# Queries and keys by seven block products instead of eight, in a transformer block on one core

## The chip, the cores and the metric

The kernel runs on one core of one Trainium2 chip, in one launch. The metric is the device time of one execution in microseconds (us), as the median of several runs. The engines are called by the names of the profile: PE (TensorE, matrix products; PEld is its weight load), DVE (VectorE), ACT (ScalarE), POOL (GpSimd), SP (SyncE, which issues nearly all transfers).

## The reference

Everything is float32. The input `h` is 8 sequences ("batches" below, b = 0 to 7) of 1024 tokens with 512 channels.

```
x = h
x = x + layernorm(attention(layernorm(x)))       # 16 heads of 32, causal
x = x + layernorm(ffn(layernorm(x)))             # 512 -> 2048 -> 512

attention:  q, v, k = split(x @ Wqvk)            # each 1024 x 512
            s = (q k^T + causal mask) / sqrt(512), per head
            wv = softmax(s) v;  result = wv @ Wo
ffn:        hidden = x @ W1 + b1
            act = relu(hidden + c * w_imag * sin(theta + 0.1 hidden) * 0.1)
            result = act @ W2 + b2                # c = cos(theta) w_real + sin(theta) w_imag
```

## The kernel before, in words

One program goes through the 8 batches one after the other. Inside a batch come attention, then the feed-forward part, and the two are interlocked: a batch's first norm, its first projections and its moments are made while the batch before is still at work. The order of instructions on every engine is the order in which the program emits them (`in_order`), and Python generators say where work is slipped in: `advance(work)` emits the next step of a generator, `finish(work)` the rest.

The normalised input of a batch lies transposed in two tiles `xnT[b, 0]` and `xnT[b, 1]`, one for each half of 512 tokens, each with four chunks (`kc`) of 128 channels. Heads are handled in four groups of four (g = 0 to 3); a group has 128 columns of queries, of keys and of values.

**Projections of a group** (`project_qkv`, line 461). Queries and keys come from `queries_or_keys(n, half)`: four matmuls of 128x512 (the four chunks) into one PSUM bank, evacuated by ACT at line 488. Four such calls make 16 matmuls (line 477). In the profile one float32 matmul is two records. Values come from `values(t0)`, line 497: eight matmuls of 128x128 for two token tiles, and an ACT copy; four calls. These steps are the filler: the attention of group g is interleaved with the projections of the group after it (after g = 3: of group 0 of the next batch).

**Attention of a group** (`attention`, line 770) has three stretches.

1. `find_maxima` (line 536) needs row maxima. It has four runs. A run is PE score matmuls (line 575), which DVE reduces straight from PSUM (lines 593 and 605). Run 0 has one unit, runs 1 to 3 have two; a unit takes four of the eight PSUM banks. After each run come filler steps, as many as `MAX_FILL` says (its first row is for g = 0). The partial maxima are cut into bf16 parts (`split`, lines 553 to 562) and transposed on PE (line 115).
2. The first part of the second pass, three units of keys for queries 0 to 511 (`at` = 0, 1, 2). At `at` 0 and 1, `later` runs the two late units of maxima, called here the late runs A and B (`MAX_LATE`). A unit of the second pass is `weigh`: bf16 matmuls that subtract the maxima (line 681), score matmuls (line 692) into four banks, an ACT exponential for each half of them (line 707), and on diagonal blocks a POOL `affine_select` (line 711). One unit later `weighted_values` (line 730) multiplies with the values.
3. The second part, seven units for queries 512 to 1023 (`at` = 3 to 9; u = 0 to 6). DVE adds up the weights (line 759), for the sums that are taken at the next group's run 0 (line 745). A filler step comes after the `weigh` of u = 5 and one after that of u = 6: they are the first two half-steps of the projections after next.

During g = 2, PE also transposes the next batch's norm (`norm1`, two tiles at `at` = 0 and 1 and at u = 5 and 6); during g = 3 the output projection (line 897) is slipped in from `at` = 4 on.

**PSUM.** `psum()` hands out banks by a fixed rule when the program is built: of the free banks or pairs, the one that was drained longest ago in program order. A unit of maxima or of the second pass takes two pairs.

**Feed-forward** (`feed_forward`, line 942) has eight steps s of seven products (line 1009) with DVE and ACT work on their results, and a second layer (line 1144) whose operands POOL prepares (line 1125); it ends with s = 7 and a tail s = 8 in which the second layer alone is left.

Of the kernel before, what the change touches and what calls it, by code (L numbers as in the profile page):

```python
# [32 lines left out]
def kernel(  # L33
# [22 lines left out]
    TPB = HALF // P  # L56
    HPG = P // HD
    NG = NH // HPG
    QSCALE = 1.0 / math.sqrt(D)

    HC = HPG // 2
    MPART = 3
# [48 lines left out]
    def in_order(instruction):  # L111
        tc.keep_in_program_order(instruction)
# [19 lines left out]
    PRODUCTS2 = ("2", "4", "1", "6", "7", "5", "3")  # L132
    w1_mixed = dram.tile([NSTEP, len(PRODUCTS), P, 2 * 2 * P], F32, tag="w1m", name="w1_mixed")
    w2_mixed = dram.tile([NSTEP, len(PRODUCTS2), P, 2 * QUART], F32, tag="w2m", name="w2_mixed")
    wqvk_v = w_qvk.rearrange("(kc p) n -> p kc n", p=P)

    def w_tile(shape, name):
# [257 lines left out]
    def norm1_first():  # L395

        dst = new_xnT(0)
        return staged(NT, *norm_stages(lambda t: xt[0, t], dst, nc.scalar.copy))

    moments_ahead = {}  # L400

    def measure_ahead(b, steps):
# [58 lines left out]
    def project_qkv(b, g):  # L461

        if g and g + 1 < NG:
            fetch(b, g + 1)
        elif g + 1 == NG and b + 1 < B:
            fetch(b + 1, 0)
        qk[b, g] = [pp.tile([P, S], F32, tag="p", name=f"{n}_{b}_{g}") for n in "qk"]  # L470
        v[b, g] = pp.tile([P, NT, P], F32, tag="p", name=f"v_{b}_{g}")

        def queries_or_keys(n, half):
            pq = psum([P, HALF])
            for kc in range(KC):
                in_order(
                    nc.tensor.matmul(  # L477
                        pq,
                        w_of[b, g, 2 * n][:, kc, :],
                        xnT[b, half][:, kc, :],  # L480
                        start=(kc == 0),
                        stop=(kc == KC - 1),
                    )
                )
# [3 lines left out]
            in_order(nc.scalar.activation(dst, pq, AF.Copy, scale=1.0 if n else -QSCALE))  # L488
            drained(pq)
            yield True  # L490

        def values(t0):
            pv = psum([P, 2, P])
            for t in (t0, t0 + 1):
                for kc in range(KC):
                    in_order(
                        nc.tensor.matmul(  # L497
                            pv[:, t - t0, :],
                            xnT[b, t // TPB][:, kc, (t % TPB) * P : (t % TPB + 1) * P],
                            w_of[b, g, 1][:, kc, :],  # L500
                            start=(kc == 0),
                            stop=(kc == KC - 1),
                        )
                    )
            in_order(nc.scalar.copy(v[b, g][:, t0 : t0 + 2, :], pv))
            drained(pv)
            yield True

        yield from queries_or_keys(0, 0)
        yield from values(0)  # L510
        yield from queries_or_keys(1, 0)
        yield from queries_or_keys(0, 1)
        yield from queries_or_keys(1, 1)
        for t0 in (2, 4, 6):
            yield from values(t0)

    MAX_RUNS = (  # L520
        (((0, 0), (2, 0)),),
# [248 lines left out]
    def attention(b, wvT, after):  # L770
# [23 lines left out]
        work = projections(0)  # L794
        for g in range(NG):
            more, first = after(g)
            mT, later = find_maxima(b, g, work, sums, more if first is None else iter(()))
            mTs = [mT]
            at = 0
            for c in range(2):  # L800
                accs = []
                total = None
                units = KEY_UNITS[c]
                for u, keys in enumerate(units):
                    later(at)
# [26 lines left out]
                    def step(accs=accs, u=u, last=u == len(units) - 1, weights=weights, c=c, g=g,  # L832
                             placed=placed, total=total, apart=c and apart, dst=wvT[c][:, g, :]):
                        if u == 0:
                            accs.append(psum([P, HALF]))
                        acc = accs[0]
                        weighted_values(acc, b, g, u == 0, last, weights, placed)
                        if apart:
                            if not last:
                                accs.append(psum([P, HALF]))  # L840
                                weight_sums(accs[1], *total, last=False)
                            weight_sums(accs[1], weights, placed, first=False, last=last)
                        if last and c:

                            def whole():
                                if apart:
                                    whole_sum = accs[1]
                                else:
                                    whole_sum = psum([P, HALF])
                                    weight_sums(whole_sum, *total)  # L850
                                divide(acc, whole_sum, dst)

                            summing[0] = whole
                        elif last:
                            nc.scalar.copy(dst, acc)
# [15 lines left out]
    def finish_block(b, half, wvT, x2T, mixed, out_w):  # L871


        x2T[half] = tp.tile([P, KC, HALF], F32, tag="t", name=f"x2T_{b}_{half}")
        mixed[half] = mixp.tile([P, 3, 2, QUART], F32, tag="mix", name=f"mix_{b}_{half}")
        ys, xns, mvs, rss = {}, {}, {}, {}

        def x(t):
# [46 lines left out]
        def mix(t):  # L925
# [6 lines left out]
            m1, m2, m4 = (mixed[half][:, n, :, t * P : (t + 1) * P] for n in range(3))  # L932
# [9 lines left out]
    def feed_forward(b, x2T, mixed, before, between):  # L942
# [49 lines left out]
        def product(bank, s, name, first=False):  # L992
# [7 lines left out]
                "4": m[:, 2],  # L1000
                "5": m[:, 0],
                "6": m[:, 1],
# [247 lines left out]
        load(WEIGHTS - 2 - KC)  # L1250
        advance(between)
        finish(before)
        units = second()
        advance(units)
        for s, quota in enumerate(SECOND):
# [3 lines left out]
            for n, more in enumerate(quota):  # L1259
# [19 lines left out]
    for _ in range(TPB):  # L1279
# [76 lines left out]
```

## Time and profile before

| | |
|---|---|
| median of 3 runs (lowest, highest) | 3681.59 us (3681.03, 3681.76) |
| the profiled execution's own time | 3681.3 us |
| its span in the trace | 3679.6 us |
| granted PE clock | 0.997 |
| PE busy | 3601.1 us, 98% |
| DVE busy | 2680.4 us, 73% |
| ACT busy | 1408.2 us, 38% |
| POOL busy | 1133.8 us, 31% |
| DMA | 476.21 MB, mean 129 GB/s |

Busy times are of one profiled execution. Its own time is 1.7 us more than its span and 0.3 us under the median. The ends of matmuls are modelled, so the starts of successive PE groups say more than their durations: what a block of matmuls takes is read from its start to the start of the next block. A batch takes about 460 us, some 230 us of it attention.

### The profile page before, as it was taken

How to read it: one execution, taken by the hardware profiler on the slowest of the kernel's cores; microseconds unless marked ns; L12 is line 12 of the kernel's file. 1: busy time of each engine (PE TensorE's matmuls, PEld its weight loads, DVE VectorE, ACT ScalarE, POOL GpSimd, SP SyncE). 2: the span in 40 equal slices, each digit the busy share in tenths (PEclk: the TensorE clock that was granted, in tenths of full speed). 3: DMA queues.
4: the chain of work that ended last, by engine and by line, in shares of the span. 5: the costliest groups of instructions: out<-in, count | busy, mean ns of one | idle time of the engine just before them, and what ended most of it. 6: DMA issues, size and time to landing. Idle time of an engine off the chain costs nothing.

```text
span 3679.6 us, 61558 instructions
## 1 busy us (share of the span) xinstructions
PE 3601.1 (98%) x22721; PEld 2357.4 (64%) x22721; DVE 2680.4 (73%) x5571; ACT 1408.2 (38%) x2708; POOL 1133.8 (31%) x1740
## 2 busy tenths in 40 slices
PE   8999999999999999999999999999999999999998
PEld 4447864478654786548854488544885458854587
DVE  5877867678676786767867678776787767777775
ACT  4552135621355213652146521465114642156410
POOL 2333432134311343113431234222342223422243
PEclk9999999999999999999999999999999999999999
DMA  4444751047510574105841068310683116820176
GB/s 137 142 141 132 243 192 34 20 146 249 175 41 10 158 258 154 41 10 172 266 132 41 13 185 269 112 41 18 198 275 92 38 33 199 262 70 13 47 220 197
DMA packets 305084, 476.21 MB, mean 129 GB/s; under 512 B 29136, under 2 KB 90640, under 8 KB 304784
## 3 DMA queue, kind: packets, MB, share of 16 engines
q1 hardware_dynamic: 302624, 470.44, 40.8%
q8 instruction: 181, 2.97, 0.3%
q10 hardware_dynamic: 2160, 1.84, 0.2%
q14 instruction: 119, 0.97, 0.1%
HBM read 440.70 MB, written 31.46 MB: 128 GB/s over the span
## 4 chain that ended last, share of the span: by engine, by line
PE 83%; DVE 11%; ACT 2%; POOL 2%; issue 1%; DMA 0%; POOLq 0%; DVEq 0%; SPq 0%; ACTq 0%
PE banks L1144 16%; PE banks L1009 15%; PE banks L477 13%; PE banks L575 8%; PE banks L730 7%; PE banks L692 7%; PE banks L497 7%; PE banks L897 6%; PE banks L681 3%; PE banks L115 2%; DVE u L1036 2%; DVE hid L1052 2%; DVE u L1030 1%; PE banks L745 1%; DVE hid L1058 1%; ACT w L707 1%
## 5 line engine op out<-in xcount | busy, mean ns | idle before, releaser
L707 ACT ACTIVATE w<-banks 128x1024 f32<-128x1024 f32 (+1 forms) x640 | 566.6, 939 | 296.1 <-PE banks L692 296.0
L759 DVE TENSOR_TENSOR w<-w 128x1024 f32<-128x1024 f32 (+3 forms) x400 | 421.9, 1099 | 186.7 <-PE banks L730 151.8
L711 POOL TENSOR_SCALAR_AFFINE_SELECT w<-w 128x256 f32<-128x256 f32 x512 | 287.3, 578 | 847.2 <-ACT w L707 839.8
L605 DVE CUSTOM_DVE_ANT_0 es<-banks,mask 128x128 f32<-128x128 f32 (+3 forms) x1024 | 432.5, 485 | 102.6 <-PE banks L575 102.6
L1009 PE MATMUL banks<-x2T,wm 128*128 128x256 f32 x2048 | 477.3, 381 | 28.1 <-DVE u L1079 13.6
L477 PE MATMUL banks<-xnT,wqvk 128*128 128x512 f32 x1024 | 481.3, 609 | 0.7 <-ACT xnT L342 0.7
L1144 PE MATMUL banks<-wm,hm 128*128 128x256 f32 x2048 | 470.4, 380 | 2.3 <-POOL hm L1125 2.3
L1037 ACT ACTIVATE u<-u 128x1024 f32<-128x1024 f32 x128 | 135.3, 1057 | 852.1 <-DVE u L1036 803.5
L1009 PEld LDWEIGHTS banks<-x2T,wm 128*128 128x128 f32 x2048 | 386.7, 190 | 91.0 <-DVE u L1079 16.8
L1144 PEld LDWEIGHTS banks<-wm,hm 128*128 128x128 f32 x2048 | 388.0, 190 | 56.4 <-POOL hm L1125 5.5
L593 DVE TENSOR_REDUCE mx<-banks 128x1 f32<-128x512 f32 (+1 forms) x384 | 309.8, 862 | 109.1 <-PE banks L575 109.1
L1144 PE MATMUL banks<-wm,hid 128*128 128x256 f32 x1536 | 357.7, 379 | 0.0
L1009 PE MATMUL banks<-mix,wm 128*128 128x256 f32 x1536 | 354.6, 380 | 2.3 <-DVE u L1079 2.3
L1125 POOL TENSOR_TENSOR hm<-hid 128x256 f32<-128x256 f32 x256 | 204.0, 797 | 456.2 <-DVE hid L1058 437.9
L477 PEld LDWEIGHTS banks<-xnT,wqvk 128*128 128x128 f32 x1024 | 182.8, 190 | 239.1 <-issue 184.5
L692 PE MATMUL banks<-q,k 32*128 32x512 f32 (+3 forms) x3072 | 329.6, 491 | 0.0
L730 PE MATMUL banks<-w,v 128*32 128x512 f32 (+3 forms) x3072 | 318.5, 495 | 5.4 <-POOL w L711 5.4
L1009 PEld LDWEIGHTS banks<-mix,wm 128*128 128x128 f32 x1536 | 291.1, 190 | 50.6 <-issue 7.6
L575 PE MATMUL banks<-k,q 32*128 32x512 f32 (+3 forms) x3072 | 322.0, 513 | 0.4 <-DVE mx L605 0.2
L1144 PEld LDWEIGHTS banks<-wm,hid 128*128 128x128 f32 x1536 | 292.4, 190 | 39.1
L625 ACT ACTIVATE es<-es,mx 128x512 f32<-128x512 f32 (+3 forms) x512 | 279.6, 550 | 2.1 <-DVE mx L605 2.1
L497 PEld LDWEIGHTS banks<-wqvk,xnT 128*128 128x128 f32 x2048 | 239.3, 192 | 51.6 <-issue 24.4
(114 smaller groups left out, 4322.9 us busy)
## 6 DMA issues: line engine op xcount, KB each, us to landing
wm<-w_mixed SPq DMA_DIRECT2D x1344, 256.0 KB, 3.1
xin<-in_L_attn_h_dram SPq DMA_DIRECT2D x112, 256.0 KB, 3.8
wqvk<-in_L_attn_Wqvk_dram SPq DMA_DIRECT2D x93, 256.0 KB, 5.2
out_dram<-x SPq DMA_DIRECT2D x64, 256.0 KB, 2.1
x<-in_L_attn_h_dram SPq DMA_DIRECT2D x60, 256.0 KB, 3.1
w_mixed<-w_t SPq DMA_DIRECT2D x56, 256.0 KB, 3.0
wo<-in_L_attn_Wo_dram SPq DMA_DIRECT2D x32, 256.0 KB, 5.0
w_t<-in_L_ffn_W_dram SPq DMA_DIRECT2D x32, 128.0 KB, 4.0
```

The lines of the kernel that those rows point to most:

```text
L477: nc.tensor.matmul(pq, w_of[b, g, 2 * n][:, kc, :], xnT[b, half][:, kc, :], start=(kc == 0), stop=(kc == KC - 1),)
L497: nc.tensor.matmul(pv[:, t - t0, :], xnT[b, t // TPB][:, kc, (t % TPB) * P : (t % TPB + 1) * P], w_of[b, g, 1][:, kc, :], start=(kc == 0), ...
L575: nc.tensor.matmul(scs[j // 2][:, j % 2, at : at + n], queries[r, i * P : (i + 1) * P], keys[r, k0 : k0 + n], start=True, stop=True,)
L593: nc.vector.tensor_reduce(out=mx[:, m], in_=sc[:, m, cols], op=ALU.min, axis=mybir.AxisListType.X,)
L605: nc.vector.tensor_tensor_reduce(out=es[:, m, cols], in0=sc[:, m, cols], in1=mask[:, HALF - n :], scale=1.0, scalar=FMAX, op0=ALU.add, op1 ...
L692: nc.tensor.matmul(sts[j // 2][:, j % 2, cols], all_keys[r, kb * P : (kb + 1) * P], all_queries[r, q0 : q0 + n], start=False, stop=True,)
L707: in_order(nc.scalar.activation(w[:, :, :width], st[:, :, :width], AF.Exp, scale=-1.0))
L711: select = nc.gpsimd.affine_select(out=square, in_=square, compare_op=ALU.is_ge, fill=0.0, base=0, pattern=[[0, 2], [1, P]], channel_multi ...
L730: nc.tensor.matmul(acc[r, HALF - n :], v[b, g][:, kb, r], weights[j // 2][:, j % 2, cols], start=first and k == 0, stop=last and k == len( ...
L759: in_order(nc.vector.tensor_add(t[:, :, q], t[:, :, q], w[:, :, cols]))
L1009: nc.tensor.matmul(bank[:, n, :], w[:, n, kc, :], moving[:, kc, :], start=first and kc == 0 and n == 0, stop=kc == 1 and n == 1, skip_grou ...
L1144: nc.tensor.matmul(region, a[:, n], w[:, n], start=start and n == 0, stop=last and n == 1, skip_group_check=True,)
```

## The change

In groups 1 to 3 of every batch, queries and keys no longer come from sixteen matmuls. The two weight blocks (queries, keys), each in two halves of channels, times the two halves of tokens, are a 2 x 2 by 2 x 2 block product of eight block multiplications with two matmuls each. It is replaced by seven block multiplications (fourteen matmuls) with sums before and after. Group 0 of each batch keeps its sixteen matmuls, in another order.

- Four sums of the weights for each group (`mix_weights_of_group`) are made once by POOL in batch 0 and stored in DRAM (`qk_mixed`); later batches fetch them, two more transfers of 256 KB for each group.
- Four differences of the input (`mix_x`) are made by POOL, eight instructions of 128x512 for each batch: for batch 0 before its attention, for the others in the last two steps (s = 7 and 8) of the feed-forward before.
- Each product is evacuated by ACT (seven evacuations of 128x512 instead of four), and POOL makes queries and keys by seven sums of 128x512 for each group (`blocks`).
- A filler step is now a whole step: values of two tiles, two products (the last of `blocks`: one product), or four matmuls. Values for the first two pairs of tiles come first, then the products, then the other values. `MAX_FILL` is one step for each run (two for run 0 of g = 0); one step follows the transposes, as before. In the second pass the steps are at `at` = 1 and 4 instead of 0 and 1, and one at u = 6 instead of at u = 5 and u = 6.
- The scale 1/sqrt(512) is split between queries and keys.
- The pool of 128x1024 tiles `pp` has 24 buffers instead of 19 and takes over the tiles of the pool `mixp`, which is gone.

```
-    QSCALE = 1.0 / math.sqrt(D)
+    HALF_SCALE = float(D) ** -0.25
...
-    pp = ctx.enter_context(tc.tile_pool(name="pp", bufs=19))
+    pp = ctx.enter_context(tc.tile_pool(name="pp", bufs=24))
...
-    mixp = ctx.enter_context(tc.tile_pool(name="mixp", bufs=2))
...
+        if b and g:
+            for n in range(2):
+                w_of[b, g, "mix", n] = w_tile([4 * P], "wmix")
+                queue.dma_start(w_of[b, g, "mix", n], qk_mixed[g, n])
...
+    def mix_weights_of_group(b, g):
...
+        pool(s12[:, near], wk[:, near], wk[:, far], ALU.add)
+        pool(s12[:, far], s12[:, near], wq[:, near], ALU.subtract)
+        pool(s34[:, near], wq[:, near], wk[:, near], ALU.subtract)
+        pool(s34[:, far], wq[:, far], s12[:, far], ALU.subtract)
+        for n in range(2):
+            nc.sync.dma_start(qk_mixed[g, n], w_of[b, g, "mix", n])
+
+    def mix_x(b):
...
+        for to, left, right in ((t1, b12, b11), (t2, b22, t1), (t3, b22, b12), (t4, b21, t2)):
+            for kc in range(2):
+                in_order(
+                    nc.gpsimd.tensor_tensor(to[:, kc], left[:, kc], right[:, kc], ALU.subtract)
+                )
+                yield True
...
-                if kc == 1:
-                    yield True
...
+        def product(w, kc0, moving, dst, sign=1.0):
+            pq = psum([P, HALF])
+            for kc in range(2):
+                in_order(
+                    nc.tensor.matmul(
+                        pq,
+                        w[:, kc0 + kc, :],
+                        moving[:, kc, :],
...
+            in_order(nc.scalar.activation(dst, pq, AF.Copy, scale=sign * HALF_SCALE))
+            drained(pq)
+
+        def blocks():
...
+            p1, p6 = pair()
+            product(wq, 0, xnT[b, 0][:, :2, :], p1)
+            product(s12, 2, t2, p6)
+            add(p6, p6, p1)
+            u2 = p6
+            yield True
+            p2, p7 = pair()
+            product(wq, 2, xnT[b, 0][:, 2:, :], p2, -1.0)
+            product(s34, 0, t3, p7)
+            subtract(queries[:, near], p2, p1)
+            add(p7, p7, u2)
+            u3 = p7
+            yield True
+            p5, p4 = pair()
+            product(s12, 0, t1, p5)
+            product(wk, 2, t4, p4)
+            add(keys[:, near], p4, u3)
+            add(keys[:, far], p5, u3)
+            add(p5, p5, u2)
+            u4 = p5
+            yield True
+            p3, _ = pair()
+            product(s34, 2, xnT[b, 1][:, 2:, :], p3, -1.0)
+            subtract(queries[:, far], p3, u4)
+            yield True
+            for t0 in (4, 6):
+                values(t0)
+                yield True
+
+        values(0)
+        yield True
+        values(2)
+        yield True
+        if g:
+            yield from blocks()
+        else:
+            for n, half in ((0, 0), (1, 0), (0, 1)):
+                queries_or_keys(n, half)
+                yield True
+            values(4)
+            yield True
+            queries_or_keys(1, 1)
+            yield True
+            values(6)
+            yield True
...
-    MAX_FILL = ((3, 2, 2, 2), (1, 2, 2, 2))
+    MAX_FILL = ((2, 1, 1, 1), (1, 1, 1, 1))
...
+            if not b and g + 2 < NG:
+                mix_weights_of_group(b, g + 2)
...
-                    if at < 2:
+                    if at in (1, 4):
                         advance(work)
...
-                    if c and u >= len(units) - 2:
+                    if c and u == len(units) - 1:
                         advance(work)
...
+        mixing_x = mix_x(b + 1) if b + 1 < B else iter(())
...
+                if s >= STEPS - 1:
+                    advance(mixing_x)
         finish(measuring)
+        finish(mixing_x)
...
     finish(first_norm)
-    advance(work, 4)
+    finish(mix_x(0))
+    mix_weights_of_group(0, 1)
+    advance(work, 2)
     prepare_parameters()
```

More of the change, by code (lines that the diff above doesn't have):

```diff
@@ L134 @@
     w2_mixed = dram.tile([NSTEP, len(PRODUCTS2), P, 2 * QUART], F32, tag="w2m", name="w2_mixed")
+    qk_mixed = dram.tile([NG, 2, P, 4 * P], F32, tag="qkm", name="qk_mixed")
     wqvk_v = w_qvk.rearrange("(kc p) n -> p kc n", p=P)
@@ L398, in norm1_first @@
         return staged(NT, *norm_stages(lambda t: xt[0, t], dst, nc.scalar.copy))
+    x_mixed = {}
+    def mix_weights_of_group(b, g):
+        for n in range(2):
+            w_of[b, g, "mix", n] = w_tile([4 * P], "wmix")
+        wq, wk = (w_of[b, g, part].rearrange("p k c -> p (k c)") for part in (0, 2))
+        s12, s34 = (w_of[b, g, "mix", n] for n in range(2))
+        near, far = slice(0, 2 * P), slice(2 * P, 4 * P)
+        pool = lambda *a: in_order(nc.gpsimd.tensor_tensor(*a))
+        pool(s12[:, near], wk[:, near], wk[:, far], ALU.add)
+        pool(s12[:, far], s12[:, near], wq[:, near], ALU.subtract)
+        pool(s34[:, near], wq[:, near], wk[:, near], ALU.subtract)
+        pool(s34[:, far], wq[:, far], s12[:, far], ALU.subtract)
+        for n in range(2):
+            nc.sync.dma_start(qk_mixed[g, n], w_of[b, g, "mix", n])
+    def mix_x(b):
+        b11, b21, b12, b22 = (
+            xnT[b, half][:, 2 * n : 2 * n + 2, :] for half in range(2) for n in range(2)
+        )
+        t1, t2, t3, t4 = x_mixed[b] = [
+            pp.tile([P, 2, HALF], F32, tag="p", name=f"xm_{b}_{n}") for n in range(4)
+        ]
+        for to, left, right in ((t1, b12, b11), (t2, b22, t1), (t3, b22, b12), (t4, b21, t2)):
+            for kc in range(2):
+                in_order(
+                    nc.gpsimd.tensor_tensor(to[:, kc], left[:, kc], right[:, kc], ALU.subtract)
+                )
+                yield True
     moments_ahead = {}
@@ L484, in queries_or_keys @@
                 )
-                if kc == 1:
-                    yield True
             dst = qk[b, g][n][:, half * HALF : (half + 1) * HALF]
-            in_order(nc.scalar.activation(dst, pq, AF.Copy, scale=1.0 if n else -QSCALE))
+            in_order(nc.scalar.activation(dst, pq, AF.Copy, scale=HALF_SCALE if n else -HALF_SCALE))
             drained(pq)
-            yield True
         def values(t0):
@@ L506, in values @@
             drained(pv)
-            yield True
[L509 to L515, printed above, removed]
+        def product(w, kc0, moving, dst, sign=1.0):
[6 more added lines that the diff above has]
+                        moving[:, kc, :],
+                        start=kc == 0,
+                        stop=kc == 1,
+                    )
+                )
+            in_order(nc.scalar.activation(dst, pq, AF.Copy, scale=sign * HALF_SCALE))
+            drained(pq)
@@ new lines, in blocks, with pair @@
+        def blocks():
+            wq, wk = w_of[b, g, 0], w_of[b, g, 2]
+            queries, keys = qk[b, g]
+            near, far = slice(0, HALF), slice(HALF, S)
+            t1, t2, t3, t4 = x_mixed[b]
+            s12, s34 = (
+                w_of[b, g, "mix", n].rearrange("p (k c) -> p k c", c=P) for n in range(2)
+            )
+            add = lambda *a: in_order(nc.gpsimd.tensor_tensor(*a, ALU.add))
+            subtract = lambda *a: in_order(nc.gpsimd.tensor_tensor(*a, ALU.subtract))
+            def pair():
+                t = pp.tile([P, 2, HALF], F32, tag="p", name="blocks")
+                return t[:, 0], t[:, 1]
+            p1, p6 = pair()
[3 more added lines that the diff above has]
+            u2 = p6
+            yield True
+            p2, p7 = pair()
[20 more added lines that the diff above has]
+                yield True
@@ L796, in attention @@
             more, first = after(g)
-            mT, later = find_maxima(b, g, work, sums, more if first is None else iter(()))
+            early = more if first is None else iter(())
+            mT, later = find_maxima(b, g, work, sums, early)
+            if not b and g + 2 < NG:
+                mix_weights_of_group(b, g + 2)
             mTs = [mT]
@@ L804, in attention @@
                 for u, keys in enumerate(units):
-                    later(at)
+                    if at < 2:
+                        later(at)
                     weights, placed = weigh(b, g, c, keys, mTs[c])
-                    if at < 2:
+                    if at in (1, 4):
                         advance(work)
@@ L874, in finish_block @@
         x2T[half] = tp.tile([P, KC, HALF], F32, tag="t", name=f"x2T_{b}_{half}")
-        mixed[half] = mixp.tile([P, 3, 2, QUART], F32, tag="mix", name=f"mix_{b}_{half}")
+        if not half:
+            mixed["last"] = pp.tile([P, 2, 2, QUART], F32, tag="p", name=f"mixl_{b}")
+        m12 = pp.tile([P, 2, 2, QUART], F32, tag="p", name=f"mix_{b}_{half}")
+        mixed[half] = [m12[:, 0], m12[:, 1], mixed["last"][:, half]]
         ys, xns, mvs, rss = {}, {}, {}, {}
@@ L931, in mix @@
             b12, b22 = right[:, :2], right[:, 2:]
-            m1, m2, m4 = (mixed[half][:, n, :, t * P : (t + 1) * P] for n in range(3))
+            m1, m2, m4 = (m[:, :, t * P : (t + 1) * P] for m in mixed[half])
             subtract = lambda *a: in_order(nc.gpsimd.tensor_tensor(*a, ALU.subtract))
@@ L999, in product @@
                 "3": x[:, 2:, QUART:],
-                "4": m[:, 2],
-                "5": m[:, 0],
-                "6": m[:, 1],
+                "4": m[2],
+                "5": m[0],
+                "6": m[1],
                 "7": x[:, :2, QUART:],
@@ L1278 @@
     advance(first_norm, TPB + 4)
-    for _ in range(TPB):
+    for n in range(TPB):
         advance(work)
```

## The prediction

> **What bounds the kernel now.** The first view is the page: engines' busy time and the chain of waits that ended last.
>
> ```profile
> PE 3601.1 (98%) x22721; PEld 2357.4 (64%) x22721; DVE 2680.4 (73%) x5571; ACT 1408.2 (38%) x2708; POOL 1133.8 (31%) x1740
> PE 83%; DVE 11%; ACT 2%; POOL 2%; issue 1%; DMA 0%; POOLq 0%; DVEq 0%; SPq 0%; ACTq 0%
> ```
>
> PE is the bound, so matmuls taken away can shorten the run, but only where PE doesn't then meet another engine. So the second view is the timeline of PE over one group (g = 1 of the fourth batch); its columns are start, duration, line.
>
> ```profile
> 1474.80 3.70 PE L477 MATMUL banks<-xnT,wqvk 128*128 128x512 f32 x8
> 1478.43 2.00 PE L575 MATMUL banks<-k,q 32*128 32x512 f32 x24
> ...
> 1489.70 2.00 PE L497 MATMUL banks<-wqvk,xnT 128*128 128x128 f32 x16
> 1491.63 1.14 PE L575 MATMUL banks<-k,q 32*128 32x512 f32 x8
> 1492.59 0.40 PE L681 MATMUL banks<-mT,minus 32*128 32x512 bf16 x4
> 1492.81 1.04 PE L692 MATMUL banks<-q,k 32*128 32x512 f32 x8
> 1493.78 2.05 PE L497 MATMUL banks<-wqvk,xnT 128*128 128x128 f32 x16
> 1495.76 1.14 PE L575 MATMUL banks<-k,q 32*128 32x512 f32 x8
> ...
> 1497.97 2.05 PE L497 MATMUL banks<-wqvk,xnT 128*128 128x128 f32 x16
> ```
>
> Starts follow each other without a hole. A step of four projection matmuls (eight records) takes 1478.43 - 1474.80 = 3.63 us, a half-step 1.91 (at u = 5: 1515.74 to 1517.65), a step of values 1495.76 - 1493.78 = 1.98. Late run A starts at 1491.63, late run B at 1495.76, and between them stand the first `weigh` (1.19) and a step of values. Third view, DVE at the same place:
>
> ```profile
> 1492.79 0.69 DVE L605 CUSTOM_DVE_ANT_0 es<-banks,mask 128x512 f32<-128x512 f32 x1 [2.46 <-PE banks L575]
> ...
> 1495.24 0.08 DVE L605 DVE_READ_ACCUMULATOR2_ANT mx<- 128x1 f32 x1
> ```
>
> DVE begins on A 0.20 after A's matmuls and is done with it 2.53 us later, at 1495.32, 0.44 before B starts. That step of values covers DVE almost exactly.
>
> Fourth, the same code without filler stands in the trace: the last batch has no projections to slip in during g = 3, nor at the end of g = 2. Its PE, and DVE's last word on its run A:
>
> ```profile
> 3383.76 1.81 PE L730 MATMUL banks<-w,v 128*32 128x512 f32 x8
> ...
> 3387.48 1.06 PE L730 MATMUL banks<-w,v 128*32 128x384 f32 x12 [0.48 <-POOL w L711]
> 3389.09 1.17 PE L730 MATMUL banks<-w,v 128*32 128x256 f32 x8 [0.56 <-POOL w L711]
> ```
> ```profile
> 3412.10 0.08 DVE L605 DVE_READ_ACCUMULATOR2_ANT mx<- 128x1 f32 x1
> ```
> ```profile
> 3414.67 1.06 PE L730 MATMUL banks<-w,v 128*32 128x512 f32 x8
> ```
>
> Without filler, PE finishes B and the `weigh` after it 3414.67 - 3412.18 = 2.49 us after DVE is done with A, and at u = 5 `weighted_values` takes 1.81 instead of 1.07: POOL's select isn't ready.
>
> **The change, part by part** (against the profiled execution's own 3681.3 us; the median is 0.3 more).
>
> *Matmuls removed.* Per group, 3 x 3.63 + 2 x 1.91 = 14.71 us become 3 x 3.63 + 1.91 = 12.80: one half-step, 1.91. Three groups in eight batches: **-45.8**. The runs themselves keep four matmuls behind them, so nothing moves there; what shrinks is the filler elsewhere.
>
> *The second pass loses its step at `at` = 0* (it goes to `at` = 4). Following the bank rule by hand, A holds two pairs and `weigh` the other two, so B takes A's own banks and waits for DVE; everything else of PE is queued behind B. In the group above: one product takes 1.91 from 1489.70, A ends at 1492.57, DVE is done 0.20 + 2.53 later at 1495.30, and 2.49 after that, at 1497.79, the `weigh` after B ends. Without the wait it would end after 1.19 + 0.96 + 1.25 at 1495.97. So **1.8** of the 1.98 that left is lost to the wait. It strikes g = 0 and 1 in eight batches, g = 3 in seven and g = 2 in the last: 24 x 1.8 = 43.2. In g = 2 of seven batches two norm transposes (0.97) still stand there, but their evacuations wait behind ACT's exponentials: about 1.1 each, 7.7. Sum **+50.9**. The step put at `at` = 4 costs its 1.98 again, already in the balance, but lets ACT get ahead: the `weigh`s after it took 1.25 to 1.33 where 1.19 is bare. I take 0.16 in each of 24 groups: **-3.8**.
>
> *At u = 5 no filler is left.* POOL's select for the unit before ends late, as in the last batch: 1.81 - 1.07 = 0.74 in g = 0 and 1 of all batches (g = 2 keeps transposes there, or had the wait before): **+11.8**. If DVE's adds don't slow the select, 0.3 each.
>
> *Run 0 of g = 0* loses 1.7 us of filler (two steps of values for a step of four and one of values). The timeline at the batch's start:
>
> ```profile
> 1418.18 2.61 PE L575 MATMUL banks<-k,q 32*128 32x512 f32 x16
> ```
>
> Run 1 takes 2.5 us to the next start instead of 1.93 already: it waits for DVE, which is still at the last quarter of the batch before and done with run 0 at 1418.75. Coming earlier, PE only waits longer. In seven batches 7 x 1.7 is not gained: **+11.9** (0 if it were).
>
> *POOL's sums.* The nearest row for a 128x512 sum is line 284; beside it stands DVE slowed by POOL:
>
> ```profile
> 128.09 1.26 POOL L284 TENSOR_TENSOR w_t<-w_t 128x512 f32<-128x512 f32 x1
> ```
> ```profile
> 1360.12 2.34 DVE L1052 SCALAR_TENSOR_TENSOR hid<-u,coef,hid 128x512 f32<-128x512 f32 x2
> ```
>
> Seven per group, 8.8 us, where POOL idles 18.8 us before `split`. In the runs, those of the second product pair end just before `split` (1486.99); the other four follow it: from 1490.35 (the last evacuation) to 1495.4, and the first selects come right behind, at 1496.2, for a `weighted_values` at about 1499.8. DVE's work from PSUM isn't slowed by POOL (L593's reductions took 2.42 beside the row above, as elsewhere). I take **0**, by the row at the place it is nearest to (DVE at reductions). No gain is possible, as nothing is taken from POOL; at the 2.24 that L284 took beside DVE's adds it would be +0.9 per group, 22. ACT's three more evacuations (0.60 each) find it idle.
>
> [...]
>
> *`mix_x`* runs in s = 7 and 8. From 1359.5 to 1381.6 DVE works without a hole on the last hidden layer, and PE waits 0.29 for it at 1383.37, so a delay of DVE there is PE's. Three sums of 1.26 at 0.4 lost per us (0.93 / 2.3): 1.5 in each of seven batches, **+10.5** (0 to 4 each).
>
> *Batch 0*: its sums of weights and input lie ahead of need (POOL from about 26 to 39 us, first used after 45), but delay small DVE instructions: **+2** (0 to 10). *Transfers*: 42 more loads and 6 stores of 256 KB, 5.2 us each on SP, tens of us ahead of use, the DMA engines 41% busy: **0**, up to 3 in batch 0, where weights crowd 18 buffers. The pool of 24 has 4 buffers held by `mix_x` and up to 3 by the former `mixp`, which leaves 17 to 20 for what 19 did: 0, or some us.
>
> Sum: -45.8 + 50.9 - 3.8 + 11.8 + 11.9 + 10.5 + 2 = +37.5, so 3681.3 + 37.5 = **3719 us**.
>
> **The rivals.** *The removed matmuls reach the end.* For it: PE 98% busy, no hole in the timeline. Against: the last batch shows the holes that come without filler. Then 3681 - 46, about 3636, with small waits 3650. The place is late run B: all else as above, the sum turns to a gain once the wait before B costs under 0.43 us per group instead of 1.8 (50.9 - 37.5 = 13.4, over 31).
>
> *POOL becomes the one waited for.* The four sums ahead of the first selects take 2.24 each beside DVE, 9 us from 1490.35; the selects come at 1500, after `weighted_values` at 1499.8, and lose 0.9 in 24 groups: 3719 + 22, about 3741. For: POOL is slowest where DVE adds. Against: at that time DVE reads PSUM.
>
> *Nearly no difference.* The select at u = 5 costs 0.3 (-7), run 0 gains half (-6), `mix_x` hides (-10) and B waits 1.4 (-10): 3719 - 33, about 3686.
>
> That the change doesn't do what it says: the products are fourteen matmuls, counted in the diff, and all feed queries and keys. I give that nothing.
>
> **How the numbers follow.** A measurement of this kernel tells 0.2%, 7 us, from no change. The forecast has 0.60, POOL as the one waited for 0.14, nearly no difference 0.10, the gain 0.16. Slower: 0.60 + 0.14, so 0.74; same 0.10; faster 0.16. The range leaves out the gain and the far ends: 3685 is the third rival's, 3752 where POOL's rival meets the upper `mix_x` in part.
>
> **What would show it.** In the changed profile: queries and keys with 14/16 of the records in three groups (1024 - 96 = 928 on lines 477 and that of `product`); run B's matmuls starting some 2.5 us after A's end, with "DVE mx" named; the DVE time of the runs as before; `weighted_values` at u = 5 at about 1.8; run 1 of g = 0 ending when it did; POOL busy near 1134 + 7 x 24 x 1.26 + 64 x 1.26, some 1430 us. It would be wrong if B starts without a wait, if run 1 of g = 0 comes 1.7 earlier, or if PE stands in the runs for queries or keys.

## The result, and the profile after

The changed kernel takes 3745.03 us (median of 4 runs, 3743.7 to 3745.82) where the kernel before takes 3681.31 in the same comparison: ratio 1.0173, interval [1.0155, 1.019], 63.7 us slower. Its profiled execution took 3744.76 us, 63.5 more than the profiled one of before; its span is 3743.0. A line of before is found again some 100 lines further down: score matmuls of the maxima 575 as 673, their DVE steps 593 and 605 as 691 and 703, `weigh` 692 as 790, selects 711 as 809, `weighted_values` 730 as 828, DVE's additions 759 as 857, queries and keys 477 as 513 (plain) and 545 (products), the feed-forward's 1009, 1052 and 1144 as 1114, 1157 and 1249.

The page of the changed kernel, busy times and the chain that ended last:

```profile
PE 3635.7 (97%) x22625; PEld 2374.7 (63%) x22625; DVE 2710.9 (72%) x5571; ACT 1448.8 (39%) x2780; POOL 1440.2 (38%) x1984
PE 79%; DVE 11%; ACT 4%; POOL 4%; issue 1%; DMA 0%; SPq 0%; POOLq 0%; DVEq 0%; ACTq 0%
```

PE has 96 records fewer and is nonetheless "busy" 34.6 us longer: its busy time is modelled and takes in part of what it stands before a bank. The chain says it better: PE's share falls from 83% to 79%, POOL's and ACT's rise from 2% to 4% each.

PE over the place of the forecast, g = 1 of the fourth batch (start, duration, line):

```profile
1518.51 1.14 PE L673 MATMUL banks<-k,q 32*128 32x512 f32 x8
1519.47 0.39 PE L779 MATMUL banks<-mT,minus 32*128 32x512 bf16 x4
1519.68 1.04 PE L790 MATMUL banks<-q,k 32*128 32x512 f32 x8
1520.54 2.40 PE L673 MATMUL banks<-k,q 32*128 32x512 f32 x7
...
1522.79 0.59 PE L673 MATMUL banks<-k,q 32*128 32x512 f32 x1
...
1524.44 2.05 PE L530 MATMUL banks<-wqvk,xnT 128*128 128x128 f32 x16
1526.42 1.06 PE L828 MATMUL banks<-w,v 128*32 128x512 f32 x8
...
1544.23 1.81 PE L828 MATMUL banks<-w,v 128*32 128x512 f32 x8
...
1546.62 2.05 PE L530 MATMUL banks<-wqvk,xnT 128*128 128x128 f32 x16
1548.60 2.12 PE L828 MATMUL banks<-w,v 128*32 128x384 f32 x24
```

and DVE at late run A:

```profile
1519.66 0.69 DVE L703 CUSTOM_DVE_ANT_0 es<-banks,mask 128x512 f32<-128x512 f32 x1 [2.40 <-PE banks L673]
...
1522.12 0.08 DVE L703 DVE_READ_ACCUMULATOR2_ANT mx<- 128x1 f32 x1
```

Run B now stands directly behind the `weigh`, at 1520.54, and its eight records of normally 1.14 us stretch to 1523.38, bank after bank as DVE drains A; DVE is done with A at 1522.20. The `weigh` behind B ends at 1524.44, 2.24 after that (2.49 was forecast). At the end of the group the `weighted_values` are long: 1.81 at u = 5, for the unit before it, and 2.12 for the last two units. In the kernel before the same two rows are

```profile
1517.65 1.07 PE L730 MATMUL banks<-w,v 128*32 128x512 f32 x8
...
1521.22 1.50 PE L730 MATMUL banks<-w,v 128*32 128x384 f32 x24
```

The waits of the changed kernel name both (line waited for, us in total, times, longest):

```profile
PEld banks L673 <- DVE mx L703: 111.7, 265, 0.8
PEld banks L828 <- POOL w L809: 45.0, 90, 4.3
```

In the kernel before these were 64.6 (136 times) and 27.8 (51 times).

**Where the 63.5 us are.** The starts of the first matmuls of each stage were set beside each other for all 32 groups and 8 feed-forwards: attention +42.4, feed-forward +21.9, start -0.8, together 63.5. Of each full group in batches 1 to 6, in us (stages that change by less than 0.1 are left out):

| stage | g = 0 | 1 | 2 | 3 |
|---|---|---|---|---|
| run 0 | -1.23 | 0 | 0 | 0 |
| run 1 | +1.23 | 0 | 0 | 0 |
| A to B | -2.09 | -2.09 | -1.83 | -2.09 |
| B to the first weighted values | +1.69 | +1.69 | +1.05 | +3.34 |
| first units of the second part (with the step at `at` = 4) | +1.98 | +1.98 | +1.98 | +1.98 |
| `weigh` of u = 5 to its weighted values | -1.15 | -1.08 | -1.67 | -0.06 |
| from there to the next run 0 | +1.18 | +0.62 | 0 | 0 |
| sum | +1.55 | +1.06 | -0.63 | +3.17 |

The order of steps alone moves 1.65 us of projections of the next batch's g = 0 from the end of g = 2 to run B of g = 3: the two columns are to be read together.

### The profile page after: what moved, and what is told of

Same layout as the page of the kernel before. It is cut to its first block, busy times and chain, and to the rows that moved or that the text cites. A ratio compares the mean times of both kernels' runs of the same rounds, so it can differ in the third digit from the quotient of the medians.

```text
span 3743.0 us, 62009 instructions
## 1 busy us (share of the span) xinstructions
PE 3635.7 (97%) x22625; PEld 2374.7 (63%) x22625; DVE 2710.9 (72%) x5571; ACT 1448.8 (39%) x2780; POOL 1440.2 (38%) x1984
## 4 chain that ended last, share of the span: by engine, by line
PE 79%; DVE 11%; ACT 4%; POOL 4%; issue 1%; DMA 0%; SPq 0%; POOLq 0%; DVEq 0%; ACTq 0%
PE banks L1249 17%; PE banks L1114 15%; PE banks L545 8%; PE banks L673 7%; PE banks L828 7%; PE banks L790 6%; PE banks L1002 6%; PE banks L530 5%; PE banks L513 3%; PE banks L779 3%; ACT w L805 2%; PE banks L114 2%; DVE hid L1157 2%; DVE u L1141 1%; POOL w L809 1%
## 5 line engine op out<-in xcount | busy, mean ns | idle before, releaser
L673 PE MATMUL banks<-k,q 32*128 32x512 f32 (+3 forms) x3072 | 375.4, 514 | 2.8 <-DVE mx L703 2.7
L828 PE MATMUL banks<-w,v 128*32 128x512 f32 (+3 forms) x3072 | 336.7, 496 | 15.6 <-POOL w L809 15.6
L790 PE MATMUL banks<-q,k 32*128 32x512 f32 (+3 forms) x3072 | 345.8, 496 | 0.0
L673 PEld LDWEIGHTS banks<-k,q 32*128 32x128 f32 x3072 | 175.6, 186 | 171.8 <-DVE mx L703 111.7
L530 PE MATMUL banks<-wqvk,xnT 128*128 128x128 f32 x2048 | 261.1, 282 | 0.0
L1114 PE MATMUL banks<-mix,wm 128*128 128x256 f32 x1024 | 241.9, 379 | 0.0
L1002 PE MATMUL banks<-wo,wvT 128*128 128x512 f32 x512 | 235.6, 600 | 3.2 <-DVE wvT L865 3.2
```

The costliest lines, as they stand in the source:

```text
L530: nc.tensor.matmul(pv[:, t - t0, :], xnT[b, t // TPB][:, kc, (t % TPB) * P : (t % TPB + 1) * P], w_of[b, g, 1][:, kc, :], start=(kc == 0), ...
L673: nc.tensor.matmul(scs[j // 2][:, j % 2, at : at + n], queries[r, i * P : (i + 1) * P], keys[r, k0 : k0 + n], start=True, stop=True,)
L790: nc.tensor.matmul(sts[j // 2][:, j % 2, cols], all_keys[r, kb * P : (kb + 1) * P], all_queries[r, q0 : q0 + n], start=False, stop=True,)
L828: nc.tensor.matmul(acc[r, HALF - n :], v[b, g][:, kb, r], weights[j // 2][:, j % 2, cols], start=first and k == 0, stop=last and k == len( ...
L1002: nc.tensor.matmul(y, wvT[:, kc, t * P : (t + 1) * P], out_w[kc], start=(kc == 0), stop=(kc == KC - 1),)
L1114: nc.tensor.matmul(bank[:, n, :], w[:, n, kc, :], moving[:, kc, :], start=first and kc == 0 and n == 0, stop=kc == 1 and n == 1, skip_grou ...
```

## The experiments

All times are medians of 2 to 11 runs; the kernel before stood at 3681.3 to 3682.4 in each comparison.

| kernel | us | ratio to before, interval |
|---|---|---|
| the changed kernel | 3745.0 | 1.0173 [1.0155, 1.019] |
| 1: steps at `at` 0 and 1 | 3703.9 | 1.006 [1.0045, 1.0075] |
| 2: `mix_x` in the tail only | 3723.3 | 1.0112 [1.0095, 1.0129] |
| 3: without POOL's sums | 3738.8 | 1.0155 [1.014, 1.017] |
| 4: the new order alone | 3754.3 | 1.0197 [1.0182, 1.0212] |
| 5: 1 and 2 | 3682.3 | 1.0002 [0.9993, 1.0011] |
| 6: 5, step at u = 5 | 3682.1 | 1.0 [0.9992, 1.0009] |
| 7: 6, weights' sums later | 3680.9 | 0.9997 [0.9988, 1.0006] |
| 8: 5 without DVE's additions | 3645.4 | 0.9901 [0.9883, 0.9919] |
| 9: 5, diagonal units inside | 3687.3 | 1.0016 [1.0007, 1.0025] |
| 10: before, diagonal units inside | 3711.2 | 1.008 [1.0066, 1.0094] |
| 11: before without DVE's additions | 3671.4 | 0.9971 [0.996, 0.9982] |

**1. The wait before late run B.** The steps of the second pass go back to where the kernel before has them:

```
-                    if at in (1, 4):
+                    if at < 2:
```

> The filler steps of the second pass go back from `at` = 1 and 4 to 0 and 1; all else is the changed kernel. Theory (the time went into the wait before late run B, whose banks DVE still reads): between A and B the 1.98 us of a step return, the wait goes, and the step at `at` = 4 costs no more. From the stage table of the changed kernel, 1.58 us in groups 0, 1 and 3 and 1.2 in group 2 come back, some 46 in all: 3699 us. Rival (POOL's sums are what PE really waits for, and the step hid nothing): the wait moves to the first weighted values, and the time stays above 3735.

41.2 us faster than the changed kernel, where the theory had some 46. By the starts of stages the gain of batches 1 to 7 lies where the theory puts it: A to B +2.09, B to the first values -1.69 (in g = 3, with the step that moved, +3.74 and -3.34), the step at `at` = 4 -1.98, so 1.55 to 1.61 for each group of g = 0, 1 and 3 and 1.14 for g = 2; nothing else moves there by more than 0.5, and the feed-forward by 0.3 over the whole run. The 5 us that are missing lie in batch 0, which gets 1.5 back instead of some 6: other stages of it grow. The step at `at` = 0 is no filler: it pays for itself by covering DVE.

**2. `mix_x` beside the last hidden layer.** All eight differences go behind s = 7:

```
-                if s >= STEPS - 1:
-                    advance(mixing_x)
+                if s == STEPS:
+                    advance(mixing_x, 2)
```

> The eight input sums for the next batch (`mix_x`) are made in s = 8 alone, two after each step, instead of from s = 7 on. Theory (they slow DVE's last hidden layer, which PE waits for): the feed-forward of each batch goes back from 214.3 to 211.2 us, seven times 3.1: 3745 - 22 = 3723 us. Rival (the feed-forward lost time to the shared buffers of `pp`, or POOL's queue in the tail is full too): 3735 to 3745.

21.7 us less, 3.1 for each of seven feed-forwards, and attention is unchanged: the whole growth of the feed-forward was `mix_x`. PE's timeline at s = 7 of the changed kernel:

```profile
1387.06 1.89 PE L1114 MATMUL banks<-mix,wm 128*128 128x256 f32 x8
1389.37 1.99 PE L1114 MATMUL banks<-mixl,wm 128*128 128x256 f32 x8 [0.42 <-DVE u L1184]
1391.20 1.03 PE L1249 MATMUL banks<-wm,hm 128*128 128x256 f32 x4
1394.09 1.99 PE L1114 MATMUL banks<-x2T,wm 128*128 128x256 f32 x8 [1.86 <-DVE hid L1184]
```

and of this one:

```profile
1381.75 1.89 PE L1114 MATMUL banks<-mix,wm 128*128 128x256 f32 x8
1383.48 1.89 PE L1114 MATMUL banks<-mixl,wm 128*128 128x256 f32 x8
1385.20 1.03 PE L1249 MATMUL banks<-wm,hm 128*128 128x256 f32 x4
1386.80 1.99 PE L1114 MATMUL banks<-x2T,wm 128*128 128x256 f32 x8 [0.57 <-DVE hid L1184]
```

From the first to the last of these starts 7.03 us against 5.05. In between, on POOL's timeline of the changed kernel:

```profile
1388.13 1.71 POOL L432 TENSOR_TENSOR xm<-xnT,xm 128x512 f32<-128x512 f32 x1
```

and beside it on DVE's:

```profile
1389.24 1.81 DVE L1157 SCALAR_TENSOR_TENSOR hid<-u,coef,hid 128x512 f32<-128x512 f32 x2
```

The same pair on DVE takes 1.41 in run 2. Each DVE instruction loses little, but all of them stand in one queue ahead of the evacuation that PE waits for: 0.42 and 1.86 where 0 and 0.57 are left.

**3. POOL's sums of the products.** The seven additions and subtractions of `blocks` are left out and ACT writes the products to `queries` and `keys`:

```
-            product(wq, 0, xnT[b, 0][:, :2, :], p1)
+            product(wq, 0, xnT[b, 0][:, :2, :], queries[:, near])
...
-            add(p6, p6, p1)
-            subtract(queries[:, near], p2, p1)
-            add(p7, p7, u2)
-            add(keys[:, near], p4, u3)
-            add(keys[:, far], p5, u3)
-            add(p5, p5, u2)
-            subtract(queries[:, far], p3, u4)
```

> POOL's seven sums for each group are left out, and ACT writes four of the products straight into queries and keys (so queries and keys are not the reference's). Matmuls, evacuations and their order are the same. Theory (these sums are hidden, as the prediction took them): 3740 to 3745 us, with the difference in batch 0 alone. Rival (POOL delays the selects of the second pass, 0.9 us in each of 24 groups): 3720 us or less.

6.2 us less, a little more than the theory's 0 to 5 and far from the rival's 25; nearly all of it is in batch 0 (4.9 in the first units of its g = 0, where POOL's selects stand behind other work); in the other batches it is some 0.06 per group. POOL's sums are hidden there, as forecast.

**4. The order without the seven products.** All groups have sixteen matmuls, in the changed kernel's order; no sums of any kind:

```
-        if g:
+        if False:
             yield from blocks()
...
-        mixing_x = mix_x(b + 1) if b + 1 < B else iter(())
+        mixing_x = iter(())
...
-    finish(mix_x(0))
-    mix_weights_of_group(0, 1)
```

> All groups keep sixteen matmuls for queries and keys, with no input or weight sums, but in the order of the changed kernel: values first, one whole step behind each run, steps at `at` = 1 and 4, one step at the end. Theory (the order is what costs, and the seven products save what was predicted): the waits of the changed kernel's stages, about 85 us, on top of 3681: 3760 to 3770. Rival (the seven products cost the time, by evacuations, banks or POOL, and the order little): under 3710.

73.1 us of attention above the kernel before, and nothing in the feed-forward; the time, 3754.3, is a little under the theory's range and far above the rival's. Set beside run 2, which differs by the seven products and their sums alone, the products bring 1.72 per group in the stages where a step got shorter (0.07 behind run 3, 1.65 behind B), of which the end of the group takes 0.1 to 0.2 back: 1.53 to 1.59 in batches 1 to 6, 30.7 over the run, because batch 0 loses some 6 us more with the products and their sums. So the 63.5 us are: order +73, products -31, `mix_x` +22.

**5. Both costs taken away.** Runs 1 and 2 together.

> The changed kernel with both earlier edits at once: steps of the second pass at `at` 0 and 1, and `mix_x` in the feed-forward's tail alone. If the two costs are independent, as their places say (one in the attention, one at s = 7 of the feed-forward), 3745.0 - 41.7 - 21.8 = 3682 us, level with the kernel before; what is then left of the seven products' saving of about 1.6 us per group goes into the waits for POOL's selects at the end of groups 0 and 1 and into run 0 of group 0. Rival: the two are not independent (POOL's sums, moved, meet something else): 3690 or more.

The two add up: 62.7 us less, where the runs alone took 41.2 and 21.7. What is left is level with the kernel before: 24 half-steps of PE work fewer, and no time gained.

**6 and 7. Can the rest be covered by moving a step?** First the one filler step at the end of a group goes from u = 6 to u = 5; then also batch 0's sums of weights go from behind the maxima to `at` = 5:

```
-                    if c and u == len(units) - 1:
+                    if c and u == len(units) - 2:
```
```
-            if not b and g + 2 < NG:
-                mix_weights_of_group(b, g + 2)
...
+                    if not b and at == 5 and g + 2 < NG:
+                        mix_weights_of_group(b, g + 2)
```

> As the run before, with the one filler step at the end of a group behind the `weigh` of u = 5 instead of u = 6. Theory: in groups 0 and 1 `weighted_values` waits at both places (together about 1.8 us in group 0 and 1.4 in group 1), the larger part at u = 5, where no filler is left; a step there covers it and leaves about 0.5 open at u = 6: 0.8 less in each of 16 groups, about 3669 us. Rival: the wait only moves, since the selects follow ACT and ACT follows PE, so that the sum of waits stays: about 3682.

> As the run before, and in batch 0 the sums of the weights of the group after next come at `at` = 5 of the second pass instead of right behind the maxima. Theory: in batch 0 the first selects stand on POOL behind a sum of weights that waits for its transfer (1.26 us of work after 4.99 of waiting), and weighted values waited 3.48 for them: about 5 us less, once. Rival: the weights then come late for the products after them, or POOL's other work in batch 0 takes the place: no change or up to 5 more.

The theory failed in run 6 and nearly so in run 7; the rivals held. In run 6 the wait of u = 5 shrinks by 0.61 (g = 0) and 0.74 (g = 1) and the next one grows by the same 0.61 and 0.74. In run 7 the early wait of batch 0 goes (2.3 us less in the first units of the second part), and the ends of its groups get 2.6 longer; 1.2 us are left of the 5. (The sum that waited for its transfer is one of the feed-forward's weights, line 288; the sums that run 7 moves are line 413's, which stood before it on POOL.) A wait for the last of a row of POOL's instructions is not covered by filler at an earlier one.

**8. What makes the selects late.** Run 5 without DVE's additions:

```
-                        add_weights(total[0], weights, placed)
+                        pass
```

> The changed kernel with both earlier edits, and DVE's sums of the weights in the second pass left out (the line of `add_weights`), so that the softmax's denominators lack all but the first term. Theory: the selects that PE waits for at u = 5 and 6 are late because POOL's affine_select is slowed while DVE adds (1.02 us against 0.41 for a select of 128x512): without the adds the waits of groups 0 and 1 shrink by 0.4 to 0.6 each, about 3660 to 3670 us. Rival: the wait is ACT's exponential and POOL's own time alone: unchanged, about 3682.

36.9 us less, more than the theory gave it: 1.82 per group in g = 0 and 1.05 in g = 1, 2.45 in g = 2 of the last batch, and 17 us in batch 0. The group of POOL's selects in run 5 (count, then busy time and mean ns of one):

```profile
L809 POOL TENSOR_SCALAR_AFFINE_SELECT w<-w 128x256 f32<-128x256 f32 x512 | 292.4, 591 | 679.2 <-ACT w L805 671.5
```

and in this run:

```profile
L809 POOL TENSOR_SCALAR_AFFINE_SELECT w<-w 128x256 f32<-128x256 f32 x512 | 205.8, 420 | 714.4 <-ACT w L805 701.9
```

The selects are of 128x256, not of 128x512 as the expectation has it. At the end of g = 0 of the fourth batch POOL's timeline in run 5 has its last six selects at 0.88 each; DVE's has its additions at the same time, and PE's the wait for the selects:

```profile
1467.34 5.26 POOL L809 TENSOR_SCALAR_AFFINE_SELECT w<-w 128x256 f32<-128x256 f32 x6 [0.66 <-ACT w L805]
```
```profile
1466.36 7.39 DVE L857 TENSOR_TENSOR w<-w 128x1024 f32<-128x1024 f32 x8 [0.30 <-POOL w L809]
```
```profile
1472.12 1.17 PE L828 MATMUL banks<-w,v 128*32 128x256 f32 x8 [0.56 <-POOL w L809]
```

At the same place in this run the six take 0.40 each, and the last `weighted_values` go through in 1.50:

```profile
1445.04 2.40 POOL L809 TENSOR_SCALAR_AFFINE_SELECT w<-w 128x256 f32<-128x256 f32 x6 [1.14 <-ACT w L805]
```
```profile
1447.66 1.50 PE L828 MATMUL banks<-w,v 128*32 128x384 f32 x24
```

**9 and 10. The units with selects between others.** The same order of units in run 5 and in the kernel before:

```
-        ((0,), (1,), (2,), (3,), (4,), (5, 7), (6,)),
+        ((0,), (4,), (1,), (5, 7), (2,), (6,), (3,)),
```

> The changed kernel with both earlier edits (3682.3 us), and the seven units of the second part in another order: keys 0, 4, 1, 5 and 7, 2, 6, 3 instead of 0, 1, 2, 3, 4, 5 and 7, 6. All computations are the same. Theory: at the end of a group PE waits for selects that share their time with DVE's additions; leaving the additions out took 36.9 us. With the units that need selects put between units that need none, every select has a unit's time more, and the waits at the ends of groups 0 and 1 (2.9 us together in a batch) go without leaving anything out: 3650 to 3662 us. Rival: POOL's selects and DVE's additions meet in any order, and the last unit is now a full one whose exponentials (1.94 us) PE has to wait for: 3682 or more.

> The kernel before with the same order of units, nothing else. It tells whether the seven products gain where the ends of groups have no wait. Theory: the kernel before covers the ends with two half-steps and waits there only 27.8 us for POOL in the whole run (the changed kernel with both edits waits more), so the order takes less here, about 10 us: 3670; the seven products then keep 10 to 20 us against it. Rival: the order takes the same here as in the run before it, and the seven products gain nothing under either order: 3655 here.

Both lose, 5.0 and 29.7 us: run 9 went as its rival had it, and both forecasts for run 10 were wrong. The selects get no more time, since `weighted_values` follows one unit behind wherever the unit stands, and there it has no filler behind it. The wait moves inside, and PE's weight loads wait 95.2 us for the selects instead of 43.9 (in run 10 90.5 instead of 27.8). PE's timeline of run 9 in g = 0 of the fourth batch:

```profile
1467.48 0.84 PE L828 MATMUL banks<-w,v 128*32 128x384 f32 x4 [0.31 <-POOL w L809]
1468.91 1.06 PE L828 MATMUL banks<-w,v 128*32 128x384 f32 x12 [0.59 <-POOL w L809]
```

Against the kernel before in the same order, however, the seven products now win 23.9 us. Why the order costs run 10 so much more than run 9 was not taken apart.

**11. The kernel before without DVE's additions**, the same edit as in run 8.

> The kernel before with DVE's sums of the weights in the second pass left out (the denominators lack all but the first term), nothing else; to be set beside the changed kernel with both edits and the same left out (3645.4 us). Theory: the kernel before has its two half-steps over the ends of groups and so gains less from it, some 10 to 20 us: 3662 to 3672; without the selects' wait the seven products then keep 17 to 27 us. Rival: it gains the same 37 us, 3645, and the seven products gain nothing even there.

11.0 us less, inside the theory's range. Run 8 is 26.0 us faster than this one: 1.64 to 1.72 for each of g = 0, 1 and 2, less 1.61 for g = 3. So at the ends of groups the removed half-steps are worth their PE time as soon as POOL's selects are quick, and with the additions in place the selects' wait swallows most of them there (23 us, in the table below). The 1.61 of g = 3 is a second loss, which quick selects don't lift: it is work that came from run 0 of the next batch's g = 0, and there its removal gains nothing (-1.23, then +1.23 again). No version that computes the reference beat the kernel before by what can be told from no change (run 7: 0.9997).

## Why the prediction was right, and where its sizes were off

The direction, the main mechanism (the wait before late run B) and the range held (3685 to 3752); 3719 was 26 us too low, mostly because three terms were too small: the end of a group, `mix_x` and batch 0. Its own terms against the runs:

| term | forecast | measured | from |
|---|---|---|---|
| 24 half-steps fewer | -45.8 | -41.3 | 24 x 1.72, runs 4 and 2 |
| wait before B, less ACT's lead | +47.1 | +41.2 | run 1 |
| selects at the end of a group | +11.8 | +23 | 8 x (1.68 + 1.19), stages |
| run 0 of g = 0 | +11.9 | +11.6 | 7 x 1.65, stages |
| `mix_x` | +10.5 | +21.7 | run 2 |
| batch 0 and what is left | +2 | +7.3 | 63.5 less the rows above |

The end of a group is worked out from the stages: a step 1.65 shorter and only 1.15 gained, then 1.18 lost, makes 1.68 in g = 0; 1.65 - 1.08 + 0.62 makes 1.19 in g = 1. The 1.65 is a step of four matmuls less one of values, 3.63 - 1.98; run 0 of g = 0 has it too.

*Matmuls removed.* Right in kind. The 1.91 was the first of two half-steps that together take 3.63; what goes in the end is the second, 1.72. 256 + 672 = 928 records stand on lines 513 and 545, as forecast.

*Late run B.* Right, and the main cost: run 1 shows it. DVE was waited for and named. The sign to look for was put wrongly in one point: B does not start 2.5 after A's end but 0.9, and stretches. The lead that ACT should gain from the step at `at` = 4 (0.16 per group) isn't there: that stage grew by the step's full 1.98.

*The end of a group.* This is the term that was too small: u = 5 waits 0.74 in g = 1, as taken from the last batch, but behind it the last unit waits too (2.12 against 1.50), which the sum left out although the rows of the last batch show it (3387.48 and 3389.09): with one filler step for two waits, the forecast counted only the uncovered one. The selects are one row on POOL, and its last entry ends late whichever `weighted_values` asks first (run 6). The forecast's "0.3 if DVE's adds don't slow the select" named the true cause; run 8 shows it.

*Run 0 of g = 0.* Right: the filler is 1.65 shorter, the stage only 1.23, and run 1 of that group takes the 1.23 back and ends when it did, so that all of the 1.65 is lost. *POOL's sums.* Right at nothing in seven batches (run 3), and POOL is busy 1440 us where 1430 was worked out.

*`mix_x`.* The failed size: 0.4 us lost for each us of POOL's work, 1.5 in a batch, where 3.1 were lost. The 0.4 is line 1052's pair in the kernel before, 2.34 beside POOL and 1.41 later in the same step: 0.93 in 2.3 us. That row, beside POOL's short instructions, gives one pair's loss. The sum also had three of the differences beside DVE's hidden layer where four stand (two from 1381.49, one each at 1388.13 and 1395.34), and it put PE's 0.29 at 1383.37 down to DVE, where the row names POOL's operands. Here one-input instructions of DVE lost too (line 1135: 2.41 for two in the changed kernel, 1.40 in run 2), and POOL's own operands for the second layer came later (PE waits 0.92 for them where it waited 0.29). The Trainium skill, "SBUF — State Buffer", section "SBUF: two separate sides", says that a DVE instruction with two SBUF inputs, or one in a two-port mode, and a POOL instruction that reads SBUF exclude each other: the one that starts second waits until the first has ended. By this rule four sums of 1.26 in seven batches could cost DVE 35 us, an estimate; 21.7 were measured. That line 1135 was slowed, with one tensor input, fits the rule only if it runs in a two-port mode, which no run here shows.

*Batch 0.* 2 us were taken, within 0 to 10; of the 7 left over, run 3 puts 4.9 on POOL's sums ahead of the first selects. The rest was not taken apart.

Of the rivals, "the removed matmuls reach the end" fell at the place that it named: B waits 1.55 to 1.61 per group, not under 0.43. "POOL waited for" gave 3741, near the result by luck: the seven sums that it charged cost nothing outside batch 0 (run 3), and what lies above 3719 comes from the three terms that were too small. "Nearly no difference" fell with its conditions: B waits more than 1.4, run 0 gains nothing, and `mix_x` isn't hidden.

## What to carry to other kernels

Where a PE-bound kernel is interlocked with another engine, work that looks like filler is cover: ask of each step what it hides, before counting its removal as a gain, and price the wait that appears by the place in the same trace where the filler is already missing. Read that place to its end: the first wait there need not be the only one, and a step moved from one wait to the next in the same queue covers nothing. A helper engine that is idle on average still costs time where its instructions and another engine's slow each other and one of the two has no slack.

## What the runs showed of the hardware

A POOL affine_select of 128x256 takes 0.40 us where DVE doesn't add (six of run 8) and 0.88 on average beside DVE's additions of two operands in SBUF (six of run 5). DVE's reductions from PSUM nearly keep their pace beside POOL (three at run B: 2.42 in the kernel before, 2.52 here beside a sum and two selects). In the changed kernel's start a small DVE instruction lasts as long as a POOL instruction; DVE's timeline:

```profile
33.69 1.30 DVE L227 TENSOR_SCALAR turns<-prm 128x16 f32<-128x16 f32 x1
```

In the kernel before it takes 0.17; here POOL makes two differences of `mix_x` from 32.47 to 34.96. No cost of it is seen there: the first score matmuls of attention come 0.8 us earlier than before.
